# Layer-0 attention: later loads ordered behind the first value return, masks filled by group, second context moved, two banks for the first queries

## The chip, the cores and the metric

One core of a Trainium2 chip runs the whole program as one launch. The metric is the device time of that launch in microseconds (us), as a median of several executions. A profile is one execution recorded by the hardware profiler. Engines are named as the profile names them: PE (TensorE matmul), PEld (its weight loads), DVE (VectorE), ACT (ScalarE), POOL (GpSimd), SP (SyncE, whose queue SPq issues nearly all DMAs here).

## The reference

Four layers run on x of shape 2x1024x256, float32. Each layer is a cross-attention onto 77 context rows and a feed-forward block, each with a layer norm before it and a residual after it. The change lies in the start of the first attention; the second attention uses the same function.

```python
x = x + _L0_xattn_ref(_layernorm(x), ctx, ctx, mask0, Wq, bq, Wk, bk, Wv, bv, Wo, bo)  # 16 heads of 16
x = x + _L0_ffn_ref(_layernorm(x), gate_w, gate_b, expert_w, expert_b)                 # 8 dense experts, top-2 weights
x = x + _L1_xattn_ref(_layernorm(x), ctx, ctx, mask1, wq, wk, wv, wo, bo)
x = x + _L1_ffn_ref(_layernorm(x), rhs)                                                # int8-like product
...
```

## The kernel before, in words

The 2048 tokens are four groups g of 512; a group is a tile of 128 partitions x 4 tokens (j) x 256. Groups 0 and 1 belong to the first batch, groups 2 and 3 to the second. An attention works on 16 token tiles `it = 4 g + j`.

The source is written once, in a natural order, and a scheduler of the framework decides in which order each engine gets its instructions. Every engine then works strictly in that order, so an instruction that waits holds up all that stand behind it. DMAs are issued by SP in its own order; each transfer also waits for the eighth one before it, whose completion counter it takes over.

The parts that matter here:

- Lines 101 to 119: constants, first tokens and transposed context are loaded; `load_tokens` (L109) loads a group's tokens and writes their numbers into column 512 with POOL.
- `mask_bias` (L240): four DVE instructions turn a mask into an additive bias, one for each group.
- `attention` (L283): loads four weights, then for each batch b makes the keys `kT` (ACT), the head-blocked keys `kblk` (POOL, L318), the values `v` (DVE, L330/L332). The values go out to DRAM as `vd` (L335) and come back in another layout as `vr` with four transfers (L343, L347); POOL spreads them to `vblk` (L351). Both batches stand ahead of any query.
- `measure`, `prepare`, `queries` (L462): layer-norm statistics of a group (DVE, POOL), normalisation (DVE, L156) and the addition of the output bias into x (POOL, L360), then transposes (PE, L175), their copies out (ACT L179, DVE L181) and the query product `pq` (PE, L370). `queries` takes its PSUM from `pside`, a pool of one bank.
- `scores` (L382): the mask bias enters PSUM as a matmul with the identity (L390), the scores are added (L397), DVE takes the row extremum (`mx`, L406), ACT the exponentials (L408), DVE their sums (L413, L414), POOL the division (L415).
- `values` (L418): transposes of the weights (L433), copies (L439, L441), product with `vblk` (L446), output product (L455), added to x by DVE (L460).
- `layer0_ffn` (L487): for each token tile two halves `pe` of four experts (PE L537, two PSUM buffers) and eight multiply-adds on DVE (L543).
- `layer1_ffn_setup` (L566): the weight `rhs` is loaded, its absolute maximum is taken with `partition_all_reduce` on POOL (L571), and seven DVE instructions quantise it (L573 to L575, L558 to L564). It depends on nothing but its load, so the scheduler may put it anywhere.

Of the kernel before, what the change touches and what calls it, by code (L numbers as in the profile page):

```python
# [22 lines left out]
F32 = mybir.dt.float32  # L23
# [43 lines left out]
def tile_layers(ctx: ExitStack, tc: tile.TileContext, a: dict, out: bass.AP):  # L67
# [32 lines left out]

    cst = cp.tile([P, C_END], F32, name="cst")
    nc.sync.dma_start(cst, a["consts"])
# [6 lines left out]
    def load_tokens(g):  # L109
        nc.sync.dma_start(  # L110
            xs[g], a["x"][g * GT : (g + 1) * GT, :].rearrange("(p j) d -> p j d", j=J)
        )
        nc.gpsimd.tensor_copy(
            tokens[g][:, :, 2 * D], cst[:, C_TOKEN + g * J : C_TOKEN + (g + 1) * J]
        )
# [3 lines left out]
    nc.sync.dma_start(ctxT, a["ctxT"].rearrange("(c p) b k -> p c b k", p=P))  # L119
# [8 lines left out]
    def rowvec(name, n=D, parts=P):  # L128

        t = cp.tile([parts, n], F32, name=f"r_{name}")  # L130
        nc.sync.dma_start(t, a[name].partition_broadcast(parts))
        return t
# [4 lines left out]
    def load_square(dst, name):  # L137
        nc.sync.dma_start(dst, a[name].rearrange("(c p) n -> p c n", p=P))
# [30 lines left out]
    def turned(g, name):  # L169

        xnT = work.tile([P, KC, GT], F32, tag="xnT", name=f"xnT_{name}")
        for c in range(KC):
            pt = pside(f"pxnT_{name}{c}")
# [61 lines left out]
    def load_mask(t, name):  # L235

        nc.sync.dma_start(t, a[name].rearrange("(g p j) k -> p g (j k)", p=P, j=J))
        return t

    def mask_bias(mb, mask, op, value=MASKED):  # L240

        for g in range(G):
            nc.vector.tensor_scalar(mb[:, g], mask[:, g], 0.0, value, op, ALU.mult)
        return mb.rearrange("p g (j k) -> p g j k", k=L)
# [38 lines left out]
    def attention(lay, wnames, bo, mask, bq=None, bk=None, bv=None):  # L283

        w4 = weight([P, 4, KC, D], f"w_{lay}")
        for i, n in enumerate(wnames):
            load_square(w4[:, i], n)
        wq, wk, wv, wo = (w4[:, i] for i in range(4))
        bo_r = rowvec(bo)
        if bq is not None:  # L290
            bcol = cp.tile([P, 2, KC], F32, name=f"bcol_{lay}")
            with nc.allow_non_contiguous_dma(reason="two bias vectors by partition"):
                for i, n in enumerate((bq, bk)):
                    nc.sync.dma_start(bcol[:, i, :], a[n].rearrange("(c p) -> p c", p=P))
            bv_r = rowvec(bv, parts=L)
        mb = mask()
        with tc.tile_pool(name=f"at_{lay}", bufs=2) as ap:
            kblk, vblk = [], []
            for b in range(NB):
# [35 lines left out]
                nc.sync.dma_start(  # L335
# [6 lines left out]
                for i in range(2):  # L342
                    nc.sync.dma_start(  # L343
# [3 lines left out]
                    nc.sync.dma_start(vr[: wide(NCH - 1), i, NCH - 1, :], vdh[i, full:, :])  # L347
# [7 lines left out]
                vblk.append(vb.rearrange("p i m h d -> p i m (h d)"))  # L355
            qTs, ss = {}, {}

            def prepare(g):
                normalize(g)
# [3 lines left out]

            def queries(g):
                xnT = turned(g, f"{lay}{g}")
                qT = ap.tile([P, KC, GT], F32, tag="qT", name=f"qT_{lay}{g}")
                for c in range(KC):
                    pq = pside(f"pq_{lay}{g}{c}")
# [13 lines left out]
            def scores(it):  # L382
# [3 lines left out]
                for c in range(KC):  # L386

                    sc = pbig(f"psc_{n}{c}")[:, :, : 4 * L]
                    for i in range(2):
                        nc.tensor.matmul(  # L390
                            sc[:, i].rearrange("p (h k) -> p h k", k=L), identb,
                            mb[:, g, j, :].unsqueeze(1).to_broadcast([P, 4, L]),
# [70 lines left out]
            for f in begin:  # L463
                f(0)

            def ahead(it):

                g, j = divmod(it, J)
                if g + 1 < G and j < 3:
# [5 lines left out]
    def layer0_attention():  # L475
        def mask():
            mb = mask_bias(mb0, load_mask(mask0, "mask0"), ALU.not_equal, -MASKED)
            for g in range(1, G):
                load_tokens(g)
            return mb  # L480
# [3 lines left out]
            mask, "L0_xattn_bq", "L0_xattn_bk", "L0_xattn_bv",  # L484
        )

    def layer0_ffn():  # L487
        ew = []
        for half in range(2):
            t = weight([P, KC, 4, D], f"ew{half}")  # L490
            for c in range(KC):
                nc.sync.dma_start(
# [6 lines left out]
        nc.sync.dma_start(gw, a["gate0T"].rearrange("(c p) e -> p c e", p=P))  # L499
        gb = rowvec("L0_ffn_gate_b", E)  # L500
        eb = cp.tile([E, D], F32, name="eb0")
        nc.sync.dma_start(eb, a["L0_ffn_expert_b"])
# [46 lines left out]
    def layer1_attention():  # L549
        attention(  # L550
            "a1", ["L1_xattn_wq", "L1_xattn_wk", "L1_xattn_wv", "L1_xattn_wo"], "L1_xattn_bo",
            lambda: mask_bias(mb1, load_mask(mask1, "mask1"), ALU.is_equal, -MASKED),
        )
# [72 lines left out]
    def layer2_attention(ctxn, ap):  # L626

        mb = mask_bias(mask2.bitcast(F32), load_mask(mask2, "mask2"), ALU.is_equal)
# [54 lines left out]
    def layer2_ffn(fp):  # L683

        wgu = []
        for nm in ("gate2T", "up2T"):
            t = weight([P, KC, E * INTER], nm)
            nc.sync.dma_start(t, a[nm].rearrange("(c p) n -> p c n", p=P))
            wgu.append(t)
        wd = weight([P, E, D], "down2T")  # L690
        nc.sync.dma_start(wd, a["down2T"].rearrange("e i h -> i e h"))
        gw = cp.tile([P, KC, E], F32, name="gw2")
        nc.sync.dma_start(gw, a["router2T"].rearrange("(c p) e -> p c e", p=P))
# [89 lines left out]
    def layer3_setup(ap):  # L783
# [7 lines left out]
        for g4 in range(KV):  # L791
            nc.sync.dma_start(
# [7 lines left out]
        nc.sync.dma_start(csk, a["ropek"].rearrange("i k d -> k i d"))  # L800
        m3 = ap.tile([P, NB, L], U8, name="m3")
        nc.sync.dma_start(m3, a["mask3"].partition_broadcast(P))
# [4 lines left out]
        for b in range(NB):  # L807
# [39 lines left out]
            for g4 in range(KV):  # L847
# [11 lines left out]
                nc.sync.dma_start(  # L859
# [5 lines left out]
    def layer3_attention(route, wq, mb3, kblk, vds):  # L865
        with tc.tile_pool(name="a3", bufs=2) as ap, tc.tile_pool(name="a3c", bufs=1) as c3:
            cs = c3.tile([P, 2, 2, J, HD3], F32, name="cs")
            for i in range(2):
                nc.sync.dma_start(
# [5 lines left out]
            for b, vd in enumerate(vds):  # L875
                vw = c3.tile([P, NC3, D], F32, name=f"vw3{b}")
                full = (NC3 - 1) * P
                nc.sync.dma_start(
                    vw[:, : NC3 - 1, :], vd[:full, :].rearrange("(m p) n -> p m n", p=P)
                )  # L880
                nc.sync.dma_start(vw[: H * L - full, NC3 - 1, :], vd[full:, :])
# [14 lines left out]
            def queries(it):  # L896
# [3 lines left out]
                nc.sync.dma_start(  # L900
# [123 lines left out]
    def layer3_ffn():  # L1024
        rw = cp.tile([P, KC, E], F32, name="rw3")
        nc.sync.dma_start(rw, a["L3_ffn_router_w"].rearrange("(c p) e -> p c e", p=P))
# [3 lines left out]
        with nc.allow_non_contiguous_dma(reason="hidden biases by partition"):  # L1030
            nc.sync.dma_start(b1c[:, :E], a["L3_ffn_b1"].rearrange("e (h p) -> p e h", p=P))
            nc.sync.dma_start(b1c[:, E], a["L3_ffn_ob1"].rearrange("(h p) -> p h", p=P))
# [88 lines left out]
        def experts():  # L1121
            outs = iter(dram_disjoint_views(out, E * 3 + 16))

            def load(n, fp, row0, rows, b2):
# [3 lines left out]
                nc.sync.dma_start(  # L1128
                    xe[:, :full], buf[row0 : row0 + full * P, :].rearrange("(m p) d -> p m d", p=P)
                )  # L1130
                if full < m:
                    nc.sync.dma_start(xe[: rows - full * P, full], buf[row0 + full * P : row0 + rows, :])
                bt = fp.tile([P, D], F32, tag="b2", name=f"b2_{n}")
                nc.sync.dma_start(bt, b2.partition_broadcast(P))
# [52 lines left out]
            with tc.tile_pool(name="f3", bufs=2) as fp:  # L1187
# [16 lines left out]
                def first(k):  # L1204
# [5 lines left out]
                    nc.sync.dma_start(w1, a["L3_ffn_w1"][e].rearrange("(c p) n -> p c n", p=P))  # L1210
                    w2 = weight([P, NH, D], f"w2_{e}")
                    nc.sync.dma_start(w2, a["L3_ffn_w2"][e].rearrange("(c p) n -> p c n", p=P))
# [16 lines left out]

                with tc.If(more > GT):  # L1230
# [9 lines left out]
    with tc.tile_pool(name="masks", bufs=1) as mp:  # L1240
# [8 lines left out]
        nc.sync.dma_start(ctxn, a["ctxn"].rearrange("b k d -> k b d"))  # L1249
        layer0_attention()  # L1250
        layer0_ffn()
# [107 lines left out]
```

## Time and profile before

| what | us |
|---|---|
| median of 3 runs (1182.38 to 1190.85) | 1182.4 |
| the profiled execution | 1185.39 |
| its span | 1183.5 |
| PE busy in the span | 1053.2 (89%) |
| DVE busy in the span | 719.0 (61%) |
| PE busy in the first 60 us | 34.0 |
| PE busy from 60 to 160 us | 98.8 |

The busy time of PE over the whole span is high, but it is not even: of the first 60 us, in which the first attention gets going, PE is busy a little over half. From 60 us on, the rest of the first attention and the first feed-forward block keep it nearly full, apart from the turn between the two around 170 us.

How to read the lines shown further down: in a table by stretches, each row has the stretch, its length, and for PE, PEld, DVE, ACT and POOL the busy time and the number of instructions; the last three columns are the granted PE clock (1.00 is full), the busy share of the DMA engines, and GB/s. In a timeline each row has the start, the busy time, the engine, the line, the operation, what it writes and reads, and the count; in square brackets stands how long the engine had been idle before it, and what it is taken to have waited for. SPq rows are DMA issues, not transfers.

### The profile page before, as it was taken

What the parts mean: (1) busy time and instruction counts of PE and PEld (TensorE: products, weight loads), DVE (VectorE), ACT (ScalarE), POOL (GpSimd) and SP (SyncE); (2) the same over time, 40 slices, a digit from 0 to 9 for tenths busy, and PEclk for the clock granted to TensorE, in tenths of its full rate; (3) what the DMA queues carried; (4) which work ended last, traced back from release to release, by engine and by line L of the source; (5) the groups of instructions that cost most, each with busy time, mean ns of one, the idle gap of its engine ahead of it and who ended that gap; (6) DMA issues with size and microseconds to landing.
All of it is one profiled execution on the core that took longest, in us unless ns stands there. A gap on an engine that the chain in (4) does not pass through costs nothing. (4 is left out here: it accounts for less than half of the span.)

```text
span 1183.5 us, 13880 instructions
## 1 busy us (share of the span) xinstructions
PE 1053.2 (89%) x4778; PEld 662.2 (56%) x4778; DVE 719.0 (61%) x1850; ACT 361.4 (31%) x1108; POOL 389.9 (33%) x370
## 2 busy tenths in 40 slices
PE   5699989999999879696988999999999649999996
PEld 3255544444455446354654655778788527667664
DVE  6778855775779967758686638767878311212211
ACT  1466620000567622231211010655457101101100
POOL 6443310014334324604040002765676331221221
PEclk9799998999999966698989999999999759999998
DMA  8500037432200012201020014222224120443430
GB/s 260 81 1 2 2 63 133 79 63 30 71 2 1 1 38 92 66 1 35 1 43 1 0 53 158 65 56 53 78 44 115 45 103 28 127 146 121 145 99 13
DMA packets 96951, 74.36 MB, mean 63 GB/s; under 512 B 57650, under 2 KB 84578, under 8 KB 96878
## 3 DMA queue, kind: packets, MB, share of 16 engines
q1 hardware_dynamic: 89582, 57.68, 17.8%
q10 hardware_dynamic: 4800, 9.46, 4.4%
q0 software_dynamic: 2496, 6.31, 1.5%
q8 instruction: 40, 0.66, 0.2%
q14 instruction: 33, 0.27, 0.1%
HBM read 54.83 MB, written 19.64 MB: 63 GB/s over the span
## 5 line engine op out<-in xcount | busy, mean ns | idle before, releaser
L408 ACT ACTIVATE s_a<-psc_a,mx_a 128x77 f32<-128x77 f32 x512 | 121.9, 337 | 63.6 <-DVE mx_a L406 61.4
L415 POOL TENSOR_TENSOR s_a<-s_a,sm_a 128x616 f32<-128x616 f32 x64 | 78.5, 1228 | 129.5 <-DVE sm_a L414 98.6
L537 PE MATMUL pe_f<-ew,xnT_f 128*128 128x512 f32 x256 | 117.2, 608 | 0.0
L1176 PE MATMUL poe_e<-w,hT_e 128*128 128x256 f32 (+1 forms) x384 | 90.3, 386 | 1.1 <-DVE ye_e L1180 1.1
L543 DVE SCALAR_TENSOR_TENSOR x<-pe_f,gate_f,x 128x256 f32<-128x256 f32 x128 | 61.8, 483 | 43.6 <-PE pe_f L537 40.9
L961 ACT ACTIVATE s_a<-s_a,mx_a 128x77 f32<-128x77 f32 x256 | 67.1, 347 | 48.5 <-DVE mx_a L959 48.5
L537 PEld LDWEIGHTS pe_f<-ew,xnT_f 128*128 128x128 f32 x256 | 48.3, 194 | 55.4 <-issue 53.5
L746 PE MATMUL po_f<-down2T,hT_f 128*128 128x256 f32 x256 | 68.2, 414 | 12.2 <-DVE x L753 12.0
L1176 PEld LDWEIGHTS poe_e<-w,hT_e 128*128 128x128 f32 (+1 forms) x384 | 66.0, 175 | 21.4 <-issue 2.4
L987 PE MATMUL po_a<-vw,PT_a 128*128 128x256 f32 (+1 forms) x320 | 76.9, 380 | 0.5 <-ACT PT_a L982 0.5
L1164 PE MATMUL ph_e<-xT_e,w 128*128 128x320 f32 x256 | 75.4, 438 | 0.2
L149 POOL TENSOR_SCALAR rstd_a<-mv_a 128x4 f32<-128x4 f32 x16 | 3.7, 236 | 201.2 <-DVE mv_a L148 199.7
L406 DVE TENSOR_REDUCE mx_a<-psc_a 128x4 f32<-128x308 f32 x128 | 57.8, 464 | 13.8 <-PE psc_a L397 8.2
L746 PEld LDWEIGHTS po_f<-down2T,hT_f 128*128 128x128 f32 x256 | 50.2, 205 | 26.9 <-DVE x L753 18.7
L733 PE MATMUL pgu_f<-xnT_f,gate2T 128*128 128x512 f32 x128 | 62.6, 611 | 2.1 <-DVE hT_f L739 1.9
L753 DVE SCALAR_TENSOR_TENSOR x<-po_f,cw_f,x 128x256 f32<-128x256 f32 x128 | 60.3, 478 | 6.2 <-PE po_f L746 3.7
L446 PE MATMUL pc_a<-PT_a,vblk_a 128*32 128x256 f32 (+1 forms) x512 | 57.9, 397 | 4.4 <-DVE PT_a L441 3.8
L987 PEld LDWEIGHTS po_a<-vw,PT_a 128*128 128x128 f32 (+1 forms) x320 | 57.5, 190 | 7.2 <-ACT PT_a L982 0.7
L733 PE MATMUL pgu_f<-xnT_f,up2T 128*128 128x512 f32 x128 | 60.1, 592 | 0.0
L433 PE MATMUL pPT_a<-cst,s_a 128*128 128x128 f32 (+1 forms) x320 | 56.9, 292 | 3.0 <-ACT PT_a L439 1.6
L1164 PEld LDWEIGHTS ph_e<-xT_e,w 128*128 128x128 f32 x256 | 47.4, 190 | 21.0 <-issue 2.7
L413 DVE TENSOR_REDUCE sm_a<-s_a 128x8 f32<-128x616 f32 x64 | 50.3, 786 | 14.6 <-ACT s_a L408 12.2
(290 smaller groups left out, 1954.5 us busy)
## 6 DMA issues: line engine op xcount, KB each, us to landing
w<-in_L_ffn_w SPq DMA_DIRECT2D x16, 1024.0 KB
rb_a<-in_relbias SPq DMA_DIRECT2D x16, 616.0 KB
buf<-none ACTq DMA_DIRECT2D x12, 769.5 KB
xe_e<-buf SPq DMA_DIRECT2D x8, 513.0 KB
vd<-vo SPq DMA_DIRECT2D x8, 308.0 KB
vw<-vd SPq DMA_DIRECT2D x2, 1152.0 KB
x<-in_x SPq DMA_DIRECT2D x4, 512.0 KB
ew<-in_L_ffn_expert_w SPq DMA_DIRECT2D x4, 512.0 KB
```

The source lines that it names most:

```text
L408: nc.scalar.activation(s[:, c, 4 * i + h, :], sv[:, h, :], AF.Exp, bias=mx[:, h : h + 1], scale=-1.0,)
L415: nc.gpsimd.tensor_tensor(s[:, c], s[:, c], bc(sm, L), ALU.mult)
L446: nc.tensor.matmul(pc[cols, c, :], vblk[g // 2][: wide(m), c, m, cols], t[: wide(m), m, :], start=(k == 0), stop=(k == 1),)
L537: nc.tensor.matmul(pe[:, i, :], xnT[:, kc, j * P : (j + 1) * P], ew[half][:, kc, i * 512 : (i + 1) * 512], start=(kc == 0), stop=(kc == KC ...
L543: nc.vector.scalar_tensor_tensor(x, pe[:, e // 2, (e % 2) * D : (e % 2) * D + D], gate[:, j, 4 * half + e : 4 * half + e + 1], x, ALU.mult ...
L733: nc.tensor.matmul(pgu[:, i, :], wgu[i][:, kc, e * INTER : (e + 1) * INTER], xnTs[g][:, kc, :], start=(kc == 0), stop=(kc == KC - 1),)
L746: nc.tensor.matmul(po[:, e // 2, (e % 2) * D : (e % 2) * D + D], hTs[g, half][:, e, j * P : (j + 1) * P], wd[:, 4 * half + e, :], start=Tr ...
L753: nc.vector.scalar_tensor_tensor(x, po[:, e // 2, (e % 2) * D : (e % 2) * D + D], cws[g][:, j, ee : ee + 1], x, ALU.mult, ALU.add,)
L961: nc.scalar.activation(sh[:, h, :], sh[:, h, :], AF.Exp, bias=mx[:, h : h + 1], scale=-1.0)
L987: nc.tensor.matmul(po, t[:w, m, :], vws[g // 2][:w, m, :], start=(m == 0), stop=(m == NC3 - 1))
L1164: nc.tensor.matmul(ph[:, h % 2, :rows], w1[:, kc, h * P : (h + 1) * P], xT[:, kc, :rows], start=(kc == 0), stop=(kc == KC - 1),)
L1176: nc.tensor.matmul(po, hT[:, h, i * P : i * P + w], w2[:, h, :], start=(h == 0), stop=(h == NH - 1),)
```

## The change

All DMAs of SP now go through `read`. Once a marker is set, `read` ties each later transfer to it: it is queued on SP behind the marked instruction (order only, no wait for its completion). In both attentions the marker is the last of the four `vr` transfers of the first batch. The tokens of groups 1 to 3 and all loads of later layers therefore stand behind the return of the first values. Besides: tokens and context are loaded ahead of the constants, and the weights in the order k, v, q, o; the mask bias is filled group by group; the second batch's context is traced with token tile 4 instead of ahead of the first query; the first group's transposes and queries use `pturn`, a pool of two banks; the first group's bias addition is traced after its queries; `ctxn` is loaded after the first attention's code.

```diff
+    ahead_of = []
+
+    def read(dst, src):
+
+        if not ahead_of:
+            return nc.sync.dma_start(dst, src)
+        with tc.issue_after(ahead_of[-1]):
+            return nc.sync.dma_start(dst, src)
+
     cst = cp.tile([P, C_END], F32, name="cst")
-    nc.sync.dma_start(cst, a["consts"])
...
     load_tokens(0)
     ctxT = cp.tile([P, KC, NB, L], F32, name="ctxT")
-    nc.sync.dma_start(ctxT, a["ctxT"].rearrange("(c p) b k -> p c b k", p=P))
+    read(ctxT, a["ctxT"].rearrange("(c p) b k -> p c b k", p=P))
+    read(cst, a["consts"])
+    number_tokens(0)
...
-        for g in range(G):
+        def fill(g):
             nc.vector.tensor_scalar(mb[:, g], mask[:, g], 0.0, value, op, ALU.mult)
-        return mb.rearrange("p g (j k) -> p g j k", k=L)
+
+        return mb.rearrange("p g (j k) -> p g j k", k=L), fill
...
-        for i, n in enumerate(wnames):
-            load_square(w4[:, i], n)
+        for i in (1, 2, 0, 3):
+            load_square(w4[:, i], wnames[i])
...
-        mb = mask()
+        mbs, mb = mask()
+        mb(0)
         with tc.tile_pool(name=f"at_{lay}", bufs=2) as ap:
             kblk, vblk = [], []
-            for b in range(NB):
+
+            def context(b):
...
-                    nc.sync.dma_start(vr[: wide(NCH - 1), i, NCH - 1, :], vdh[i, full:, :])
+                    ins = read(vr[: wide(NCH - 1), i, NCH - 1, :], vdh[i, full:, :]).ins
...
             def prepare(g):
                 normalize(g)
-                nc.gpsimd.tensor_tensor(
-                    xs[g], xs[g], bo_r.unsqueeze(1).to_broadcast([P, J, D]), ALU.add
-                )
+                mb(g)
+                add_bias(g)
 
             def queries(g):
-                xnT = turned(g, f"{lay}{g}")
+                bank = pturn if g == 0 else pside
+                xnT = turned(g, f"{lay}{g}", bank)
...
             begin = (lambda g: measure(g, f"{lay}{g}"), prepare, queries)
-            for f in begin:
-                f(0)
+            measure(0, f"{lay}0")
+            normalize(0)
+            ins = context(0)
+            queries(0)
+            add_bias(0)
+            then(ins)
 
             def ahead(it):
 
                 g, j = divmod(it, J)
+                if it == 4:
+                    context(1)
                 if g + 1 < G and j < 3:
                     begin[j](g + 1)
...
     def layer0_attention():
         def mask():
-            mb = mask_bias(mb0, load_mask(mask0, "mask0"), ALU.not_equal, -MASKED)
+            return mask_bias(mb0, load_mask(mask0, "mask0"), ALU.not_equal, -MASKED)
+
+        def then(ins):
+            ahead_of.append(ins)
             for g in range(1, G):
                 load_tokens(g)
-            return mb
+                number_tokens(g)
...
             "a1", ["L1_xattn_wq", "L1_xattn_wk", "L1_xattn_wv", "L1_xattn_wo"], "L1_xattn_bo",
             lambda: mask_bias(mb1, load_mask(mask1, "mask1"), ALU.is_equal, -MASKED),
+            ahead_of.append,
         )
```

## The prediction

> **What bounds the kernel now.** I read the table of 40 slices first, then busy time by stretch, then the timeline of the first 60 us. The chain that ended last is of no use here: it names only the last microseconds.
>
> ```profile
> 36.00:48.00 12.00, 7.56 (x34) 3.40 (x33) 4.30 (x11) 5.49 (x19) 1.95 (x1) 0.93 0.80 74
> 48.00:60.00 12.00, 7.41 (x33) 3.31 (x37) 11.76 (x22) 5.20 (x19) 9.31 (x7) 0.76 0.01 1
> 60.00:80.00 20.00, 20.00 (x130) 10.55 (x126) 13.35 (x33) 13.59 (x51) 8.60 (x8) 1.00 0.00 1
> ```
>
> From 60 us PE is full, and it stays so through most of the attention: time won in the start is won at the end only as far as PE becomes full earlier, with the same work behind it. Up to 60 us PE is idle for 26.0 us. The timeline tells why:
>
> ```profile
> 18.18 0.32 SPq L335 DMA_DIRECT2D vd_a<-v_a  x1
> 35.98 0.43 SPq L343 DMA_DIRECT2D vr_a<-vd_a  x1
> 38.34 4.78 SPq L1032 DMA_DIRECT2D b1c<-in_L_ffn_ob  x1
> 40.90 1.95 POOL L571 PARTITION_ALL_REDUCE rhs<-rhs  x1 [6.13 <-DVE sm_a L414]
> 48.24 1.01 DVE L243 TENSOR_SCALAR mask<-mask 128x308 f32<-128x308 int32 x4 [4.92 <-DMA mask<-in_mask]
> 50.69 1.21 POOL L415 TENSOR_TENSOR s_a<-s_a,sm_a 128x616 f32<-128x616 f32 x1 [7.83 <-DVE mx_a L406]
> 50.80 1.74 DVE L575 RECIPROCAL rhs<-rhs 128x256 f32<-128x256 f32 x1
> 50.94 3.39 PE L370 MATMUL pq_a<-xnT_a,w_a 128*128 128x512 f32 x4 [7.38 <-DVE xnT_a L181]
> 51.86 2.49 POOL L351 TENSOR_TENSOR vblk_a<-vr_a,cst 128x640 f32<-128x640 f32 x2
> ```
>
> The values go out at 18.18 and are fetched back only at 35.98, since 16 loads of later layers stand between them on SP. Worse: DVE sits 4.92 us behind a mask of layer 2 and then spends 49 to 59 us on quantising `rhs` of layer 1. PE waits with it (7.38 us) and runs its next product at half clock (3.39 us; the same product took 1.98 at 38.21).
>
> **The start after the change**, walked by the changed program's order with durations of these rows.
>
> (1) Return of the values. Without `ctxn` ahead, mask 0 lands some 0.5 us earlier than 11.77 (154 KB at about 310 GB/s), near 11.2. Filling "by group" changes nothing: the scheduler still puts three fills ahead of the copy of the turned tokens and the fourth behind it. So 4.16 (fills) + 0.65 (copy) + 0.40 bring v to 16.4, against 16.9. From vd to vr, at 275.92 and 278.67 in layer 1, is 2.75 us, and four vr issues take 1.84: vr lands about 21.5, and SP is free for the tokens of group 1 at 21.1.
>
> (2) The price: those tokens were issued at 8.81. A load of this size took 4.6 us from issue to first use at the start (1.19 to 5.81, with one load ahead); I take 4.2, so 25.3. In the new order DVE takes one maximum (about 20.5) and then stands at the statistics of group 1: an idle 4.3 us, with everything else of the softmax queued behind.
>
> (3) DVE. Up to the wait for mask 2, DVE had done 30.4 us of work in 43.3 us. The new order holds exactly the same work (four groups' norms, eight fills, two v, two copies, nine maxima, four sums) in front of its third token tile. Its idle times: 4.9 (first tokens), 1.6 (rstd), 1.3 (mask 0), 4.1 (until the first scores, where two banks for `pq` save 0.8 us that DVE does not feel), 4.3 from step 2, 1.5 small ones: 17.7. Sum 48.1, against 49.3 before (the end of the fills of mask 2). Gain 1.2 us.
>
> (4) Beyond it, DVE no longer does the `rhs` work of 6.6 us (0.24, 1.74, 1.42, 1.32, 0.80, 1.04) and POOL has the first `vblk` (2.49) behind it. But PE was idle only 9.1 - 7.3 = 1.8 us between 50.94 and 60; no more than that can be won. The half clock stays: PE is less than half busy from 25 to 48 in the new order too. Start: -3.0 us. Bounds: -9 (group 1 lands by 21, PE at full clock) and +2 (PE fills later because the query product of group 2 moves behind).
>
> Covered: the second batch's context (POOL 2 x 2.5 us, DVE 0.4) is hoisted by the scheduler to right behind the first queries, and its vd stands on SP among layer 1's loads. SP comes to it near 30 us, v is there at 28. Mask 1 and the second vr follow 5.6 MB of loads: at some 330 GB/s from 23 us they land at 40 to 42, and DVE and POOL come to them at 43 and 45. If that cover of 3 us goes, DVE stands there as it did for mask 2. Loads of layers 1 to 3 have over 200 us of cover; the order k, v, q, o and the late bias addition (POOL 2.17) lie in time in which POOL waits for vr.
>
> **Where the removed work goes.** `rhs` and mask 2 are not gone. Their loads now stand behind the marker of layer 1, so the reduction and the seven DVE instructions are issued in the last group of the first feed-forward block, between the multiply-adds of its second token tile. Before, that stretch was clean:
>
> ```profile
> 275.92 0.33 SPq L335 DMA_DIRECT2D vd_a<-v_a  x1
> 278.67 0.39 SPq L343 DMA_DIRECT2D vr_a<-vd_a  x1
> 280.85 2.50 POOL L351 TENSOR_TENSOR vblk_a<-vr_a,cst 128x640 f32<-128x640 f32 x2 [3.15 <-DMA vr_a<-vd_a]
> 289.23 7.03 PE L537 MATMUL pe_f<-ew,xnT_f 128*128 128x512 f32 x16
> 292.87 2.04 DVE L543 SCALAR_TENSOR_TENSOR x<-pe_f,gate_f,x 128x256 f32<-128x256 f32 x4 [2.93 <-PE pe_f L537]
> ```
>
> PE is full, and DVE waits 1 to 3 us for each half tile of 3.6 us. In the clock of the run before: both query products now stand ahead of `pv`, which ends at 278.1 (before 273.9). v follows at 278.6, vr by the same delays lands by 284.9, `vblk` ends at 286.2. The reduction needs whatever made POOL idle for 6.13 us at its first use, then 1.95: 294.3. DVE, which is strictly in order, stands there with the multiply-adds behind it. Until the PSUM buffer of the half tile is free it then needs 0.66 + 1.74 + 1.01 (mask 2) + 1.42 + 0.41 + 1.32 + four times 0.48 = 8.5 us: 302.8. PE from 278.1: 3.6 + 3.6 + 0.6 + 1.0 + 3.6 + 1.9 + 1.0 + 3.6 + 1.9 = 20.8, so it wants that buffer at 298.9. Stall 3.9, less 1 because POOL is not working next to these DVE instructions (they ran beside POOL before): 3 us. The stall vanishes if the reduction is done by 291.
>
> Is that 6.13 us a fixed price? The row blames DVE, which had nothing to do with `rhs`; POOL then sat another 7.83 us after the reduction, 1.3 us longer than DVE's `sm` (49.36) explains. The Trainium skill, GPSIMD Engine Reference, "1.1 Terminology", says that kernel libraries of GpSimd are loadable and that an instruction fetches one by DMA while the program runs. If so, the wait moves with the reduction into the feed-forward block and speaks against the change: +3. If POOL was only waiting for the late load of `rhs` (issued at 26.19), the new place costs 0. The changed order shows an unnamed instruction on POOL on either side of the reduction, as before; I take the load.
>
> After a stall PE may drop to half clock:
>
> ```profile
> 173.00:174.00 1.00, 0.84 (x4) 0.30 (x4) 1.00 (x5) 0.06 (x1) 0.17 (x1) 0.64 1.09 146
> 183.00:184.00 1.00, 1.00 (x2) 0.05 (x1) 0.00 (x0) 0.00 (x0) 0.00 (x0) 0.74 0.75 85
> 53.00:54.00 1.00, 1.00 (x3) 0.30 (x2) 1.00 (x3) 0.39 (x2) 1.00 (x2) 0.60 0.00 0
> ```
>
> After four thin microseconds (169 to 173) PE was at half clock for 10 us, nearly 9 of them busy; at 50.9 it was back after 2.7. By TensorE: Matmul & The Clock Gate, "What's actually happening", about 3.4 us of sustained work bring the clock back, which would cost 1.7 us; the row at 183 makes it 5. I take 2, near the shorter one, since PE is full before and after. Tail: +5.0 us, bounds 0 and +10.
>
> Elsewhere the two orders differ by a few neighbours only; in the thin stretches from 420 to 560 us I allow 2 us either way. Sum: -3.0 + 5.0 = **+2 us**. The profiled run (1185.39) lies 3.0 above the median; I put the difference on the median: **1184 us**, about 1187.4 for a profiled run.
>
> **The rivals.** *A, near balance* (0.62): as above, 1178 to 1191. *B, the start pays and the tail is covered* (0.20): group 1 lands as DVE comes to it (-4.2), PE restarts at full clock (-1.4), and no library load stands before the reduction: -3.0 - 4.2 - 1.4 = -8.6, 1174; with all of DVE's 4.92 + 6.6 us realised, 1171. For it: the long waits removed are real; against it: step 3, the same DVE work is only shifted. *C, the tail stall decides* (0.18, slower): the reduction waits 7.83 rather than 6.13 (+1.7), PE stays at half clock for the 10 us of row 183 (5), the start wins nothing: 3 + 1.7 + 5 = +9.7, 1192. It begins to decide once the reduction ends later than 291 on the clock above. That the change does not do what it says holds for one part: the fills are not spread.
>
> **How the numbers follow.** A measurement of this kernel can tell about 1% (11.8 us) from no change. Below 1170.6 lies about half of B: 0.10. Above 1194.2 lie the upper half of C and an edge of A: 0.14. The range 1173 to 1194 leaves out a tenth at each end.
>
> **What would show it.** vr issued near 19 us and `vblk` before 25; a DVE wait of some 4 us for the tokens of group 1; the third tile's maxima near 48; PE full from about 55. In the feed-forward block, a POOL gap of about 6 us before the reduction, a DVE wait for it, a PE gap of about 3 us on `pe`, then half clock. It is wrong if PE is full well before 50 us, or if the reduction finds POOL ready at once.

## The result, and the profile after

| | before | after |
|---|---|---|
| median, us | 1186.62 (1182.38 to 1192.16, 4 runs) | 1214.57 (1212.09 to 1217.41, 4 runs) |
| the profiled execution, us | 1185.39 | 1212.09 |
| its span, us | 1183.5 | 1210.3 |
| PE busy in the span, us | 1053.2 | 1065.4 |
| mean granted PE clock | 0.937 | 0.925 |

The changed kernel takes 1.0235 of the time of before (95% interval 1.0202 to 1.0268): slower by 28 us, where +2 us was forecast. Before itself took from 1180.0 us (mean clock 0.943) to 1197.1 us (0.932) in the series measured beside the experiments, so each experiment is given as a ratio to before's runs of its own series. Of the 26.8 us between the two spans, 12.2 are the same matmuls taking longer at a lower clock, and 14.6 are PE standing idle.

The first view is busy time by stretch, as shown of before. Columns: stretch, length, busy time and count for PE, PEld, DVE, ACT and POOL, granted PE clock, DMA share, GB/s.

```profile
36.00:48.00 12.00, 8.16 (x28) 4.03 (x28) 7.64 (x15) 3.31 (x13) 9.65 (x8) 0.70 0.58 160
48.00:60.00 12.00, 7.91 (x36) 3.52 (x36) 7.84 (x19) 8.18 (x29) 5.76 (x5) 0.72 0.00 1
60.00:80.00 20.00, 20.00 (x124) 10.28 (x124) 12.99 (x31) 12.39 (x45) 6.08 (x5) 1.00 0.00 1
320.00:340.00 20.00, 14.01 (x52) 5.62 (x49) 12.96 (x31) 10.86 (x46) 8.35 (x7) 0.66 0.15 52
```

PE is busy 0.6 us longer from 36 to 48 than before and yet does less: the clock there is 0.70 against 0.93. It is full from 60 us, as before. The last row has no counterpart in the prediction at all: in the first tiles of layer 1's attention PE is busy 14 of 20 us at 0.66, where before has this:

```profile
320.00:340.00 20.00, 19.65 (x132) 10.55 (x130) 14.34 (x32) 15.61 (x58) 6.95 (x6) 1.00 0.01 1
```

**Where the time went.** To place the loss, each PE product is compared with the same product in the profiled run of before (same line, same operands, the same occurrence), and the difference of the two starts is taken as the median over 20 us of before's time. The table has it for every kernel that was run; minus is earlier. Each row is one profiled execution set against the one of before, so small differences between rows say little.

| kernel | at 140 | at 240 | at 360 | at 440 | at 540 | at 900 | at 1140 |
|---|---|---|---|---|---|---|---|
| after | +4.9 | +3.6 | +19.6 | +16.5 | +23.6 | +26.6 | +26.3 |
| mask 1 later | -2.8 | -4.5 | +12.4 | +10.0 | +18.7 | +20.6 | +19.2 |
| tokens first | -4.8 | -5.9 | +11.4 | +9.1 | +17.7 | +19.3 | +17.8 |
| one bank in layer 1 | +4.0 | +2.7 | +11.5 | +7.5 | +16.2 | +17.3 | +20.8 |
| two banks, queries held | +3.5 | +2.1 | +12.8 | +10.7 | +17.7 | +21.1 | +22.5 |
| before, two banks in layer 1 | +1.1 | -0.4 | +5.0 | +1.7 | +1.8 | +3.8 | +7.2 |
| reduction in the turn | +5.3 | +4.8 | +10.7 | +10.6 | +22.1 | +12.9 | +14.9 |
| before, reduction in the turn | +1.2 | -2.5 | -2.5 | -4.9 | +16.5 | +16.4 | +16.8 |
| POOL order | +5.3 | +4.1 | +19.2 | +16.3 | +23.7 | +26.5 | +26.5 |
| all undone | -2.1 | -3.1 | -3.1 | -4.4 | +2.5 | +5.5 | +3.6 |
| tokens first, one bank | -4.7 | -6.1 | -5.8 | -7.0 | +10.3 | +13.3 | +14.2 |
| tokens first, two banks in layer 0 | -7.0 | -9.6 | -9.5 | -10.7 | -0.1 | +3.4 | +5.3 |
| the same, with POOL order | -7.5 | -10.0 | -10.0 | -11.2 | -6.2 | -3.9 | -2.6 |

For the changed kernel: some 4 us in the start, 16 between 240 and 360, a net 4 between 360 and 540, 3 between 540 and 900. A rise of 1 to 3.5 between 540 and 900 is in eleven of the thirteen rows, and before's profiled run (1185.39) lies below the median of each of its later series, so the last 3 are not laid on the change. *Reduction in the turn* wins 9.2 us back there; no run shows why.

**The start.** This is the timeline of the changed kernel (start, busy time, engine, line, operation, count, and in brackets the idle time ahead of it with what ended it):

```profile
19.02 1.81 SPq L106 DMA_DIRECT2D vr_a<-vd_a  x4
...
21.18 2.50 POOL L367 TENSOR_TENSOR vblk_a<-vr_a,cst 128x640 f32<-128x640 f32 x2 [6.17 <-DMA vr_a<-vd_a]
...
24.86 1.40 DVE L159 BATCH_NORM_STATS2 bns_a<-x 128x6 f32<-128x256 f32 x4 [3.63 <-DMA x<-in_x]
...
37.92 0.43 SPq L108 DMA_DIRECT2D mask<-in_mask  x1
...
45.04 3.16 DVE L255 TENSOR_SCALAR mb<-mask 128x308 bf16<-128x308 int32 x4 [3.70 <-DMA mask<-in_mask]
...
48.83 0.46 DVE L429 TENSOR_REDUCE mx_a<-psc_a 128x4 f32<-128x308 f32 x1
...
52.09 0.67 PE L413 MATMUL psc_a<-mb,identb 128*128 128x308 bf16 x2 [6.01 <-ACT s_a L431]
...
54.02 3.41 PE L393 MATMUL pq_a<-xnT_a,w_a 128*128 128x512 f32 x4
```

The values come back and the tokens land as forecast. Then DVE comes to the four fills of mask 1 at 41.34 (45.04 less 3.70), and the mask, issued at 37.92, lands only at 45.0. The softmax of layer 0 is queued behind them: from 41.34 to 48.2 DVE does nothing else, PE idles 6.01 us, and its next query product still takes 3.41 us, half clock. One wait for a later layer's mask was removed from the start, and another took its place.

**Layer 0's last feed-forward group.** The same view, of POOL, DVE and PE:

```profile
286.69 2.51 POOL L367 TENSOR_TENSOR vblk_a<-vr_a,cst 128x640 f32<-128x640 f32 x2 [4.98 <-DMA vr_a<-vd_a]
...
292.79 1.88 PE L393 MATMUL pq_a<-xnT_a,w_a 128*128 128x512 f32 x4
...
297.40 1.95 POOL L604 PARTITION_ALL_REDUCE rhs<-rhs  x1 [8.20 <-issue]
...
298.80 1.88 PE L393 MATMUL pq_a<-xnT_a,w_a 128*128 128x512 f32 x4
...
299.39 0.42 DVE L606 TENSOR_TENSOR rhs<-rhs 128x256 f32<-128x256 f32 x1 [8.53 <-POOL rhs L604]
...
305.64 5.37 PE L569 MATMUL pe_f<-ew,xnT_f 128*128 128x512 f32 x8 [4.96 <-DVE x L575]
...
308.03 2.39 POOL L334 TENSOR_TENSOR kblk_a<-kT_a,cst 128x616 f32<-128x616 f32 x2 [8.67 <-issue]
```

POOL, DVE and PE stand one behind the other, as foreseen: 8.20 us before the reduction, DVE 8.53 us for it, PE 4.96 us for DVE, then a half tile at partly half clock (5.37 us instead of 3.6).

**Layer 1's first tiles.** PE of the changed kernel, then of before. The scores of layer 1 start at 320.30 and at 305.56:

```profile
318.59 1.88 PE L393 MATMUL pq_a<-xnT_a,w_a 128*128 128x512 f32 x4
320.30 0.43 PE L413 MATMUL psc_a<-mb,identb 128*128 128x308 bf16 x2
...
325.87 0.43 PE L413 MATMUL psc_a<-mb,identb 128*128 128x308 bf16 x2 [3.33 <-ACT s_a L431]
...
328.25 0.67 PE L413 MATMUL psc_a<-mb,identb 128*128 128x308 bf16 x2 [0.91 <-ACT s_a L431]
328.85 1.40 PE L420 MATMUL psc_a<-kblk_a,qT_a 64*128 64x308 f32 x4
...
331.98 0.67 PE L413 MATMUL psc_a<-mb,identb 128*128 128x308 bf16 x2 [1.11 <-ACT s_a L431]
```

```profile
305.56 0.43 PE L390 MATMUL psc_a<-mb,identb 128*128 128x308 bf16 x2
...
307.73 1.98 PE L370 MATMUL pq_a<-xnT_a,w_a 128*128 128x512 f32 x4
310.39 0.66 PE L175 MATMUL pxnT_a<-cst,x 128*128 128x128 f32 x4 [0.68 <-ACT qT_a L379]
...
314.72 1.98 PE L370 MATMUL pq_a<-xnT_a,w_a 128*128 128x512 f32 x4
```

Between the first scores, where PE waits for ACT's exponentials, before has group 1's second query product (307.73), then transposes (from 310.39) and the first product (314.72) of group 2. The changed kernel has none of them there. It made group 1's two products at 292.79 and 298.80, in the feed-forward block, where PE was full, and group 2's, which follow them in the same bank, ahead of the scores too (product at 318.59). With the filler gone, PE idles 3.33, 0.91 and 1.11 us and falls to half clock: its four score products take 1.40 us instead of 0.79.

The change does this through the banks. In before one side bank serves group 0's and group 1's transposes and queries of layer 1 in turn. With group 0 on the other pool the side bank is free earlier, and group 1's two products both come ahead of the last three half tiles. The second bank was meant for layer 0's first queries, but `attention` is one function for both layers.

### The profile page after: what moved, and what is told of

Read it like the earlier page. It is cut to its first block, busy times and chain, and to the rows that moved or that the text cites. A ratio compares the mean times of both kernels' runs of the same rounds, so it can differ in the third digit from the quotient of the medians.

```text
span 1210.3 us, 13882 instructions
## 1 busy us (share of the span) xinstructions
PE 1065.4 (88%) x4778; PEld 669.1 (55%) x4778; DVE 720.1 (59%) x1850; ACT 362.1 (30%) x1108; POOL 388.8 (32%) x370
## 3 DMA queue, kind: packets, MB, share of 16 engines
q0 software_dynamic: 2496, 6.31, 1.4%
## 5 line engine op out<-in xcount | busy, mean ns | idle before, releaser
L781 PE MATMUL po_f<-down2T,hT_f 128*128 128x256 f32 x256 | 68.2, 414 | 12.2 <-DVE x L788 12.0
L781 PEld LDWEIGHTS po_f<-down2T,hT_f 128*128 128x128 f32 x256 | 50.2, 206 | 26.8 <-DVE x L788 18.7
```

Of the source, the lines that this page charges most:

```text
L781: nc.tensor.matmul(po[:, e // 2, (e % 2) * D : (e % 2) * D + D], hTs[g, half][:, e, j * P : (j + 1) * P], wd[:, 4 * half + e, :], start=Tr ...
```

## The experiments

### What the second bank does in layer 1

*Before, two banks in layer 1*, and *one bank in layer 1* for the changed kernel:

```diff
+                bank = pturn if g == 0 and lay == "a1" else pside     # before, two banks in layer 1
-                bank = pturn if g == 0 else pside
+                bank = pturn if g == 0 and lay == "a0" else pside     # after, one bank in layer 1
```

> The kernel before, with nothing changed but that the first group's transposes and queries of the SECOND attention use the two-bank pool. Theory F (filler): the free single bank lets the transposes and query products of group 1 slip into the last group of the first feed-forward block, where PE is full; they cost their 4 us there, and the first tiles of the second attention, which wait for ACT and DVE, lose the work that kept PE busy and its clock up. Then this alone is slower than before by 4 to 9 us (before 1186.6; so 1190 to 1196), and the PE gap between the first score tiles of layer 1 shows half clock behind it. Rival S (stall): what follows 300 us in the changed kernel is only the aftermath of the stall on rhs and of the half clock that it leaves; then two banks do nothing here: within 2 us of before.

> The changed kernel, with one bank again for the first queries of the second attention (two stay in the first attention). Theory F: 7 to 9 us come back: 1205 to 1208 (changed kernel 1214.6, before 1186.6), although the stall on rhs in the feed-forward block is still there. Rival S: the stall decides, so 1213 to 1216.

Measured: 1.0052 (1.0027 to 1.0077), median 1195.26 against 1189.99; and 1.0121 (1.0059 to 1.0184), median 1205.39. In the table the bank alone costs before 5.4 us between 240 and 360 (-0.4 to +5.0), and taking it from the changed kernel leaves 8.8 of the 16 us there. Both went as the theory of the pulled products has it. The rival, that only the stall on `rhs` and what it leaves behind count, falls: before has no such stall and loses 5.4 us.

But a second bank could also hurt in another way. *Two banks, queries held* keeps both banks and puts only the two products of group 1 back, one behind the feed-forward block and one behind the first scores:

```diff
+            def late(lay, g, c):
+                if lay == "a1" and g == 1:
+                    return tc.issue_after(held[("f03", 3) if c == 0 else "a100"])
+                return nullcontext()
...
+                        with late(lay, g, c):          # around each query product
...
```

> The changed kernel, with two banks in both attentions, but the two query products of group 1 in layer 1 are queued on PE behind the last half tile of the feed-forward block and behind the first scores, which is where the kernel before has them. Theory (pulled filler): what the second bank costs around 260 to 345 us is only that these two products run where PE is full anyway and are missing between the first scores: this run gives back the same 7 to 8 us that one bank gave back (1205.4), so 1205 to 1208, ratio about 1.014, and the gap of 3.33 us before the third pair of score products is gone. Rival (the banks themselves, or the reduction's stall alone costs the 16 us): as the changed kernel, 1213 to 1216, ratio 1.023.

Measured: 1.0122 (1.0073 to 1.017), median 1205.61: the same as with one bank. PE's timeline of this kernel has the filler again, group 2's transposes included, and the gap of 3.33 us is gone:

```profile
304.47 11.99 PE L576 MATMUL pe_f<-ew,xnT_f 128*128 128x512 f32 x24 [8.69 <-DVE x L582]
...
318.01 0.43 PE L420 MATMUL psc_a<-mb,identb 128*128 128x308 bf16 x2
...
320.18 1.99 PE L400 MATMUL pq_a<-xnT_a,w_a 128*128 128x512 f32 x4
322.83 0.66 PE L188 MATMUL pxnT_a<-cst,x 128*128 128x128 f32 x4 [0.68 <-ACT qT_a L409]
...
326.08 0.43 PE L420 MATMUL psc_a<-mb,identb 128*128 128x308 bf16 x2 [0.38 <-ACT s_a L438]
```

So it is the place of these products that costs 5 to 7 us: between 240 and 360 this run loses 10.7 us and the one with one bank 8.8, the changed kernel 16.0. By the medians (1205.61 and 1205.39) two banks cost nothing by themselves. The first row also tells what the reduction costs without the pulled products to bridge it: PE stands 8.69 us.

### The reduction and mask 2

The reduction is tied to the turn between the first attention and the first feed-forward block, where POOL is idle, its DVE part and the fills of mask 2 to group 1 of that block. This was done once in the changed kernel, which has them in the block's last group, and once in before, which has them in its start. In the changed kernel the second marker had to go as well, since the load of `rhs` stands behind it, so the loads of the later layers are sent earlier too (`rhs` at 42.38). No run separates the two, but the waits seen in that stretch lead to the reduction.

```diff
+        with tc.issue_after(held["f03"]):
             nc.gpsimd.partition_all_reduce(am, rw, P, bass_isa.ReduceOp.absmax)
...
+        with tc.issue_after(held["f01", 1]):      # the seven quantising instructions on DVE
...
+        with tc.issue_after(held["f01", 2]):      # the fills of mask 2
...
-            ahead_of.append,                      # in the changed kernel alone
+            lambda ins: None,
```

> The changed kernel, with the reduction of rhs queued on POOL behind the norm of the first feed-forward block's last group and its DVE part behind the second token tile of group 1; mask 2 is filled behind the third. PE has work for both there. The order of POOL at the turn to layer 2's feed-forward comes out as before the change, too (the square root of group 0 ahead of the second group's two long products). Theory F: the stall of 6.8 us in the last group goes, and 4 us at the turn to layer 2's feed-forward; the pulled queries keep their 9: 1214.6 - 10.8 = 1204. Rival S: the half clock behind the stall goes with it: 1214.6 - 6.8 - 9 - 4 = 1195.

> The kernel before, with the same move of rhs and mask 2 to the middle of the first feed-forward block; nothing else changed by hand. The 4.92 us wait for mask 2, the library wait on POOL and 6.6 us of DVE work leave the first 60 us. If the start of the kernel before is really bound by them, 5 to 9 us are gained there; the scheduler now puts the second group's two long products on POOL ahead of group 0's square root at the turn to layer 2's feed-forward, as in the changed kernel: +4 if that order is worth what the traces say. Sum 1186.6 - 7 + 4 = 1183.6. If the start is bound by something else: 1190.6.

Measured: 1.0072 (1.0034 to 1.011), median 1198.76; and 1.0103 (1.0048 to 1.0157), median 1201.85. In the changed kernel 10.1 of the 16 us are gone; the 5.9 that remain (+4.8 to +10.7) are about what the pulled products cost alone. What the two causes leave when the other is removed, 8.8 and 5.9, makes 14.7; what goes with each, 10.1 and 7.2, makes 17.3: they cover the 16.

Before with the same edit missed both expectations, and it is the more useful run. It has no wait for mask 2 and no `rhs` work in its start, which is what the change set out to reach, and it is only 2.5 us earlier at 240. It then loses 21 us between 440 and 540, in a stretch whose lines the edit does not touch. Its busy time by stretch there, and that of before for the same stretches:

```profile
436.00:448.00 12.00, 11.67 (x43) 7.35 (x43) 11.93 (x32) 2.81 (x6) 7.11 (x8) 0.50 0.05 13
448.00:460.00 12.00, 12.00 (x40) 7.92 (x39) 8.58 (x26) 1.16 (x2) 5.53 (x7) 0.50 0.30 94
460.00:472.00 12.00, 11.53 (x46) 8.43 (x45) 6.03 (x7) 2.97 (x7) 4.24 (x4) 0.50 0.28 87
472.00:484.00 12.00, 11.44 (x37) 7.55 (x36) 5.14 (x13) 3.45 (x7) 0.00 (x0) 0.50 0.28 81
```

```profile
436.00:448.00 12.00, 9.36 (x42) 6.90 (x43) 11.22 (x32) 2.38 (x5) 7.51 (x11) 0.50 0.22 83
448.00:460.00 12.00, 11.68 (x33) 5.97 (x32) 10.30 (x30) 2.33 (x4) 6.74 (x8) 0.50 0.25 79
460.00:472.00 12.00, 11.96 (x79) 9.60 (x78) 7.13 (x18) 3.29 (x7) 4.80 (x4) 0.86 0.40 123
472.00:484.00 12.00, 10.03 (x47) 6.25 (x46) 8.87 (x27) 6.98 (x14) 3.61 (x3) 0.85 0.60 179
```

From 448 to 472 PE is busy over 11.5 of each 12 us in both. In before the clock comes back between 460 and 472, in the other it stays at 0.50 to 484 and beyond. A further 3.7 us is PE's gap in front of layer 2's feed-forward block, 11.72 us here and 8.03 in before, as the expectation had it.

### The start

*Mask 1 later* ties the four fills of mask 1 into the first feed-forward block; *tokens first* lets the tokens of groups 1 to 3 go ahead of the marker, so that only the loads of later layers stand behind it.

```diff
         def fill(g):
-            nc.vector.tensor_scalar(mb[:, g], mask[:, g], 0.0, value, op, ALU.mult)
+            with tc.issue_after(held["f00", 1]) if mb is mb1 else nullcontext():
+                nc.vector.tensor_scalar(mb[:, g], mask[:, g], 0.0, value, op, ALU.mult)
```

```diff
         def mask():
-            return mask_bias(mb0, load_mask(mask0, "mask0"), ALU.not_equal, -MASKED)
+            mask = load_mask(mask0, "mask0")
+            for g in range(1, G):
+                load_tokens(g)
+                number_tokens(g)
+            return mask_bias(mb0, mask, ALU.not_equal, -MASKED)

         def then(ins):
             ahead_of.append(ins)
-            for g in range(1, G):
-                load_tokens(g)
-                number_tokens(g)
```

> The changed kernel; only the four fills of the second attention's mask bias are queued behind the second token tile of the first feed-forward block on DVE (no other instruction changes its place on any engine but two neighbours). In the changed kernel DVE stands 3.70 us for that mask and 3.16 us at its fills, from 41.3 to 48.2, and PE is idle for 6.0 us beside it. If that stop is what made the start 4 us worse instead of 3 us better, 4 to 6 us come back: 1.023 of before falls to about 1.019. If the stop covers for something else that is late (the second vr, the tokens of group 1, half clock), as the middle placement of rhs suggested (it took 11 us of waits and work out of the start of the kernel before and the start gained 2.5), then at most 2 us: 1.022.

> The changed kernel, with the loads of the tokens of groups 1 to 3 ahead of the marker again (as before the change). DVE's 3.63 us wait for group 1 goes; vr and the first vblk come about 4 us later. If the tokens' lateness costs the start its gain, 3 to 4 us come back (1.020); if the later stop at mask 1 takes it up, nothing (1.023); if the early vr was worth something, it gets worse.

Measured: 1.0152 (1.0083 to 1.022), median 1205.41; and 1.0157 (1.0084 to 1.0229), median 1204.29. Each gave more than expected: 8.1 and 9.5 us at 240. In both, PE is full or nearly so from 48 us on (12.00 and 11.59 of 12), 12 us sooner than in before. Busy time by stretch of *tokens first*:

```profile
36.00:48.00 12.00, 9.64 (x48) 4.61 (x47) 8.95 (x21) 7.05 (x25) 7.54 (x6) 0.98 0.42 100
48.00:60.00 12.00, 11.59 (x72) 5.49 (x71) 8.30 (x19) 9.62 (x39) 6.47 (x6) 1.00 0.00 1
```

The wait for mask 1 goes in both, though the second run leaves the fills where they were. With the tokens there DVE has other work first and comes to the fills at 45.97, when the mask has landed, and does them without a wait:

```profile
45.97 0.99 DVE L255 TENSOR_SCALAR mb<-mask 128x308 bf16<-128x308 int32 x4
```

The fills took 3.16 us beside POOL's `vblk` in the changed kernel. The two edits remove one wait in two ways, so their gains do not add: both together, in the last row of the table and with the other edits of that row, are 13.6 us earlier at 240 than the changed kernel, not 17.6.

### The turn to layer 2's feed-forward block

In the changed kernel PE waits 12.04 us in front of the transposes of layer 2's feed-forward block, in before 8.03. POOL does the second group's update first (from 509.45), ahead of the last step of the statistics that these transposes need (515.26); before has that step first (490.21, the update from 491.27). *POOL order* pins before's order:

```diff
-            for k in range(len(chain) + 1):
-                if k < len(chain):
-                    chain[k](0)
+            for k in range(len(chain)):
+                chain[k](0)
...
             route(0)
+            chain[-1](1)
...
+            with tc.issue_after(held["f20"]) if g == 1 else nullcontext():     # the product with gamma
```

> The changed kernel; at the turn to layer 2's feed-forward POOL takes the square root of group 0 before the second group's product with gamma (2.34 us) and its addition (2.17 us), as it did before the change; nothing else moves by hand. Theory: PE's 12.04 us gap there becomes the 8.03 us of before: 4 us less, 1.020 of before. Rival: the gap is only filled by the next wait (DVE normalises o of group 1 in front of x of group 0): 1 us or less, 1.023.

Measured: 1.0235 (1.0164 to 1.0306), median 1213.56: nothing. The transposes of before, of after, and then of this run:

```profile
493.81 1.45 PE L175 MATMUL pxnT_f<-cst,x 128*128 128x128 f32 x4 [8.03 <-DVE x L156]
```

```profile
517.24 1.45 PE L187 MATMUL pxnT_f<-cst,x 128*128 128x128 f32 x4 [12.04 <-DVE x L168]
```

```profile
514.99 0.48 PE L188 MATMUL pxnT_f<-cst,x 128*128 128x128 f32 x1 [7.96 <-DVE x L168]
...
518.47 0.47 PE L188 MATMUL pxnT_f<-cst,x 128*128 128x128 f32 x1 [1.70 <-DVE x L168]
```

The gap is the forecast 4 us shorter, but PE comes to it 1.8 us later, and it now waits for each piece of DVE's normalisation. So the first transpose comes 2.25 us sooner, and the four end at 518.9 instead of 518.7.

### All of it undone, and what beats both

*All undone* is the changed kernel with one bank in both attentions, the reduction in the turn, and its DVE part, mask 2 and mask 1 in the first half of the feed-forward block; what is left is the early return of the values, the loads ordered by the first marker and the late context of the second batch. The second marker is gone here and in the runs below.

> The changed kernel with the causes removed together: one bank for the first queries again (both attentions), rhs reduced and quantised in the middle of the first feed-forward block with mask 2, mask 1 filled in its first group. The order on POOL and DVE at the turn to layer 2's feed-forward comes out exactly as before the change. What stays: the values' early return, the late second context, the ordered loads. By the sum of the causes (16 from 260 to 345 us, 4 at the turn, 4 to 7 in the start) the changed kernel's +28 all goes: 0.997 of before (0.993 to 1.003). If the ordered loads cost something by themselves, it stays above 1.005.

Measured: 0.9998 (0.9971 to 1.0024), median 1187.73 against 1188.57. The offset is flat from 240 to 360: none of the 16 us is left, so the reduction and the pulled products are the whole of it. It leads by 4.4 us at 440 and is 2.5 us late at 540.

The last three runs add the tokens first to this kernel. The second keeps two banks for layer 0 alone, the third also pins POOL's order.

> Tokens of groups 1 to 3 ahead of the marker, mask 1 filled in the feed-forward block, rhs and mask 2 in the middle of it, one bank in both attentions. Theory: the start keeps what the early return of the values can give without the two waits it bought, -4 to -5 us against before at 150 us, nothing is lost from 260 to 400 us: 1182 to 1186 where before is 1187.5, ratio about 0.997. Rival (the start is worth nothing at the end, since the thin stretch from 430 to 520 us gives it back as in the run with all undone): 1188, ratio 1.000.

> As the run before it, but with the two banks kept for the first queries of layer 0 alone, as the change's words say. Theory: the two banks save another 1 to 2 us in the start and pull nothing in layer 1: start -5 to -6 us, 1181 to 1185 where before is 1187.5, ratio about 0.996. Rival: as the run with one bank, or the same as before, ratio 1.000.

> As the run before it (two banks for the first queries of layer 0 alone, tokens first, mask 1, mask 2 and rhs in the feed-forward block), and POOL's order at the turn to layer 2's feed-forward block pinned: the statistics of group 0 ahead of the second group's normalisation, as before has it. There the run before it lost 7 of its lead of 10.7 us in a PE gap of 12.96 us in front of the transposes of the second group of tokens, where before has 8.03. Theory (the order makes the gap): the gap falls to 8 to 10 us and 3 to 4 us of the lead are kept: ratio 0.992 to 0.994. Rival (as when the same pin was tried on the changed kernel: the next wait fills what is won): ratio 0.996 again.

Measured: 1.0098 (1.006 to 1.0135), median 1201.4: missed, with the lead of 7.0 us at 440 turned into a delay of 10.3 at 540. Then 0.9963 (0.9945 to 0.9982), median 1186.07 against 1191.43. Then **0.9921 (0.9888 to 0.9954)**, median 1180.96 against 1192.14. At 240 the tokens ahead of the marker are worth 3.0 us (-3.1 to -6.1), and the second bank in layer 0, which the prediction thought of no use to DVE, another 3.5. The last two runs beat both kernels, the third by most, and here the pinned order does pay. The transposes of the second and the third of these runs:

```profile
490.15 1.44 PE L188 MATMUL pxnT_f<-cst,x 128*128 128x128 f32 x4 [12.96 <-DVE x L168]
...
493.18 1.06 PE L774 MATMUL pgu_f<-xnT_f,gate2T 128*128 128x512 f32 x1
```

```profile
485.98 0.48 PE L188 MATMUL pxnT_f<-cst,x 128*128 128x128 f32 x1 [9.19 <-DVE x L168]
...
489.45 0.48 PE L188 MATMUL pxnT_f<-cst,x 128*128 128x128 f32 x1 [1.70 <-DVE x L168]
...
491.51 3.00 PE L775 MATMUL pgu_f<-xnT_f,gate2T 128*128 128x512 f32 x4
```

The products after the transposes start 1.67 us sooner. Most of the other 4 of the 6 us at 540 is clock, in these two executions at least (1191.20 and 1183.52 us, where the medians are 1186.07 and 1180.96): the same stretch in the second run and in the third reads

```profile
496.00:502.00 6.00, 6.00 (x20) 4.31 (x20) 1.96 (x12) 1.48 (x2) 0.00 (x0) 0.50 0.00 0
```

```profile
496.00:502.00 6.00, 6.00 (x19) 3.00 (x19) 5.30 (x25) 2.59 (x5) 2.88 (x3) 1.00 0.00 0
```

with PE busy all of it at 0.50 in one and at 1.00 in the other. From 496 to 508 the clocks are 0.65 and 1.00, an estimated 4.2 us of work.

## Why the prediction was wrong

The step that failed is the sentence "Elsewhere the two orders differ by a few neighbours only", with its allowance of 2 us either way. The neighbours were the two query products of group 1 in layer 1, moved, with group 2's behind them, from a place where PE waits to one where it is full. That cost 5 to 7 us: 5.3 by *two banks, queries held*, 7.2 by *one bank in layer 1*, 5.4 by the bank alone in before. The prediction saw that group 0's second product had moved ("both query products now stand ahead of `pv`") and dated the values by it, but did not look where group 1's went, nor what had filled PE in the place that they left.

The second failed step is "Covered", and with it the start of -3.0, which came out as +3.6. Its own condition named what happened: "If that cover of 3 us goes, DVE stands there as it did for mask 2". It was no small risk: DVE arrived at 41.3 instead of 43, and the mask at 45.0 instead of 40 to 42. The fills then took 3.16 us beside POOL's `vblk`, a neighbour that the prediction allowed for elsewhere. When the fills are moved away, the start is 4.5 us earlier than before, so the rest of the walk holds:

- Step 1: `vr` issued at 19.02 (forecast near 19), v on its way at 16.37 (16.4), `vblk` at 21.18 (before 25).
- Step 2: the tokens' wait is 3.63 us and ends at 24.86 (4.3, at 25.3).
- Step 3: the third tile's first maximum starts at 48.83 (48.1). The size is right by luck: the wait of 3.70 us for mask 1 stands in it, which the sum did not have.
- Step 4: "The half clock stays: PE is less than half busy from 25 to 48 in the new order too". Half of this came true: at 54.02 the query product takes 3.41 us, but from 25 to 48 PE is busy 13.42 of the 23 us. The quoted row of before, 0.93 from 36 to 48, already spoke against a half clock there. With the tokens late, group 1's two products move from 33.92 and 38.21 to 41.40 and 54.02, and the clock of that stretch fell to 0.70; with the tokens early it is 0.98.

The tail had the right mechanism with a size too small. Forecast +5.0: a stall of 3 and 2 of clock. Measured in the changed kernel: 4.96 of PE standing and 1.8 on the next half tile (5.37 less 3.6), thus 6.8. POOL waited 8.20 us before the reduction rather than 6.13, 2.1 more, about the 2.0 by which the stall passed the forecast 3. The held queries show that even this was softened by the pulled products: without them the stall is 8.69, and by the runs that isolate it the tail costs 8.8 to 10.1.

On what POOL waits for before the reduction, the Trainium skill's GPSIMD Engine Reference, "1.1 Terminology" (libraries are fetched at run time), was the reading taken. The runs agree that the wait goes wherever the reduction goes. With the reduction in the turn it is 5.98 us in before and 6.31 in the fastest kernel:

```profile
178.25 1.96 POOL L573 PARTITION_ALL_REDUCE rhs<-rhs  x1 [5.98 <-issue]
```

```profile
169.88 1.96 POOL L608 PARTITION_ALL_REDUCE rhs<-rhs  x1 [6.31 <-issue]
```

`rhs` had been sent for 150 and 135 us earlier. The rival reading, that POOL was only waiting for the load, falls with that. In the changed kernel the load is issued at 287.32, ten microseconds before the reduction, so part of the 8.20 may be the load's. No run shows a fetch itself.

Of the rivals, C's 9.7 us for the tail agrees with what the isolating runs give, though not in its parts: it had a stall of 4.7 and a half clock of 5, where 8.69 was measured with the queries held, and 1.8 in the changed kernel. It had nothing for the start or for layer 1. B's premise, a start that pays, holds once one more wait is gone (*mask 1 later*), and B lacked what happens in layer 1.

**What stays open.** Between 360 and 540 the changed kernel loses a net 4 us, and the others between 4 and 19, except before with two banks, which gains 3. The forecast allowed 2 for the thin stretches there. Order explains part of it in one case (12.96 to 9.19 us). *All undone* loses 7 us between 440 and 540 with a gap of 8.41, close to before's. Its clock comes back later than before's, and it was not settled what decides this; no run moves the clock alone.

## What to carry to other kernels

When an edit frees a buffer, ask which later work the scheduler will draw forward into it, and what filled the place that this work leaves: matmuls that bridged a wait are worth more there than in a full stretch. Behind every wait that is removed, compare the arrival of the engine with the landing of the *next* load that stands in its order, and count on no margin as thin as the 3 us that were used up here. A function that serves two layers makes every edit twice.

## What the runs showed of the hardware

- PE stayed at half clock for long while nearly fully busy: over 11.4 of each 12 us from 436 to 484 at 0.50 in one run. The forecast weighed 1.7 against 5 us for one recovery, from the Trainium skill's TensorE: Matmul & The Clock Gate, "What's actually happening" (about 3.4 us of sustained work bring the clock back) and the row at 183. In this stretch neither comes out, and no run here shows what keeps the clock down.
- Around the partition reduction POOL stood idle for 16.9 us in the changed kernel, besides its 1.95: 8.20 before it, and 8.67 after it, for which the profile names no releaser. The keys that the next instruction reads had been ready since 289.9, 18 us before it started.
- Of the four mask fills in the changed kernel the first two took 0.32 us each, the last two, beside POOL's `vblk`, 1.39 and 1.38. In *tokens first* all four took 0.30, although POOL's bias addition ran beside three of them; there the addition took 2.87 us instead of 2.17. In the one case DVE was slowed, in the other POOL.
